# Moving transposes of a four-layer graph network from TensorE to HBM round trips, and scalings from VectorE to GpSimd

## The chip, the cores and the metric

One core of a Trainium2 chip runs the whole program. The metric is the time of one execution in microseconds (us), the median of several runs. All runs told here are of the fast state; the profile of each kernel is one further execution.

The engines are named as the profile names them: PE is TensorE (PEld its weight loads), DVE is VectorE, ACT is ScalarE, POOL is GpSimd, SP is SyncE. SPq and ACTq are the queues from which SP and ACT issue DMAs.

## The reference

Sixteen graphs (a "batch" below is one of them) of 1024 nodes with 128 features, one 1024x1024 adjacency matrix each, go through four layers, each of them `x = x + layer(relu(layernorm(x)))`.

```python
# layer 0, three times: h = h @ W + b; nh = h / |h|
#   h = (adj * (nh @ nh.T)) @ h, with relu but for the last
# layer 1: two matmuls around adj.T @ h
# layer 2:
h = x @ W;  s1 = h @ a[:f];  s2 = h @ a[f:]
alpha = tanh(s1[:, :, None] + s2[:, None, :])
attn = softmax(where(adj > 0, alpha, -1e15), axis=-1);  out = attn @ h
# layer 3: e = (h @ A) @ h.T, made symmetric; softmax over adj > 0, times adj;
#   then gates: z = sigmoid(i * h' + f * x);  out = o * tanh(z)
```

## The kernel before

The kernel records operations with estimated durations and latencies, and a list scheduler puts them in order, engine by engine, by priorities that were tuned by hand or by search (`LEADS`). Each engine then takes its instructions strictly in that order. Two or three batches are in work at once.

```python
# the scheduler's latency from an operation's end to its users, us
LATENCY = {"PE": 0.2, "DVE": 0.185, "ACT": 0.2, "POOL": 0.12, "DMA": 4.0}

# layers 0 and 3: one row of blocks of a symmetric product
pc, view = square.row(j, s)        # PE: above the diagonal matmuls, below it transposes of kept blocks
... scalar_tensor_tensor(ew, pc * rn * aT[j]) ...     # DVE reads PSUM
square.keep(j, s, pc)              # ACT (or DVE) copies the blocks that are mirrored later

# layer 2: the score s1 along the free axis, on all partitions
for s, (lo, hi) in enumerate(HALVES):
    p1 = ps(f"p1_{b}_{s}")
    # four transposes of h's score column, broadcast to 128 columns, then an eviction by ACT
    nc.tensor.transpose(cols(p1.t, c - lo), h.t[:, at : at + 1].to_broadcast([P, P]), ident)
    evict(p1, s1, lo, hi)
# the score's column is then used again, for the softmax's sums
dve(TINY, [], [h], lambda: nc.vector.memset(by_block(h.t, E2)[:, :, D : D + 1], 1.0))
for j in range(NB):
    act(..., lambda: nc.scalar.activation(e.t, s1.t, AF.Tanh, bias=<score s2 of node block j>))
    ...

# layer 3: exp of a row times the adjacency, on DVE in two halves
nc.vector.tensor_mul(span(e.t, lo, hi), span(e.t, lo, hi), span(aT[j].t, lo, hi))
```

Of the kernel before, what the change touches and what calls it, by code (L numbers as in the profile page):

```python
# [53 lines left out]
class Plan:  # L54
# [53 lines left out]
    def link(self):  # L108



        for o in self.ops:
            for b in [b for b in o.new if b.kind == "ps"]:
                for r in b.users:
                    if r is not o:
                        for t in [t for t in r.new if t.kind not in self.psum]:
                            r.new.remove(t)
                            o.new.append(t)
        behind = {o: set(o.preds) for o in self.ops}
        for o in self.ops:  # L120
            for b in o.new:
                for u in b.users:
                    if u is not o:
                        self.place_after(u, o)
                        behind[u].add(o)
        for o in self.ops:
            for b in [b for b in o.new if b.kind in self.psum]:
                for u in b.users:
                    for p in behind[u]:
                        if p.seq < o.seq:  # L130
                            self.place_after(o, p)
        for o in reversed(self.ops):
            o.tail = o.us + max((s.tail + o.lat for s in o.succs), default=0.0)
            o.rank = (self.deadline(o.batch) - o.tail - self.leads.get(o.key, 0.0), o.seq)
# [87 lines left out]
def tile_adj_preln(  # L222
# [97 lines left out]
    for load_it in first:  # L320
# [11 lines left out]
    POOLS = {"adjT": 16, "adjL": 5, "x": 3, "big": 13, "above": 2, "got": 1, "bank": 8, "small": 24, "row": 5, "hbm": 3}  # L332
    KINDS = {
        "adjT": ("adjT", 16, 16), "adjL": ("adjL", 5, 5), "x": ("x", 3, 3), "w4": ("big", 9, 8),
        "chunk": ("big", 10, 4), "above": ("above", 2, 1), "got": ("got", 1, 1), "ps": ("bank", 4, 4),
        "acc": ("bank", 8, 5), "small": ("small", 16, 6), "row": ("row", 5, 5), "hbm": ("hbm", 3, 2),
    }
    PERIOD, LAST, AHEAD, WINDOW = 66.0, 23.0, 2, 0.05

    LEADS = {  # L340
        "0 ACT hT": 3.5, "0 ACT hn": 18.5, "0 DVE hn": 14.5, "0 DVE nb": -43.5, "0 DVE st": -4, "0 PE ps": 13.5,
        "0 POOL rstd": -24, "00 ACT above": 74, "00 ACT hTn": -86, "00 ACT params": -0.5, "00 ACT sq": 49,
        "00 DMA by": 16.5, "00 DMA got": 16.5, "00 DVE above": -7.5, "00 DVE ew": 1, "00 DVE h": -224.5,
        "00 DVE params": 64.5, "00 DVE ss": 12.5, "00 PE acc0": -62, "00 PE ps": 81.5, "00 PE psP": 523.5,
        "00 PE sq": -15, "00 POOL rn": -26.5, "01 ACT above": 69, "01 ACT hT": 19, "01 ACT hTn": -158,
        "01 ACT sq": 4.5, "01 DMA by": 18.5, "01 DMA got": 31, "01 DVE above": 1.5, "01 DVE ew": 316.5,
        "01 DVE h": 20, "01 PE ps": 12, "01 PE psP": 27, "01 PE sq": 55.5, "01 POOL rn": 19, "02 ACT above": -1,
        "02 ACT hTn": -32, "02 ACT sq": -30.5, "02 DMA by": 21, "02 DVE above": -1, "02 DVE ew": -53.5,
        "02 DVE h": 3, "02 DVE ss": -403, "02 DVE x": -30, "02 PE acc0": -29.5, "02 PE ps": -131.5,
        "02 PE psP": 13, "02 PE sq": -24.5, "02 POOL rn": 20, "1 DMA adjL": -497, "1 DVE adjL": 4.5,  # L350
        "1 DVE hn": 238, "1 DVE mv": 35.5, "1 DVE nb": -17, "1 DVE st": -449, "1 DVE x": -3.5,
        "1 PE acc1": -32.5, "1 PE py": -31.5, "1 PE py2": -32, "1 POOL rstd": -28, "2 ACT e2": -33.5,
        "2 ACT h": 2, "2 ACT hfl": -64, "2 ACT hn": -370, "2 ACT hnT": -5.5, "2 ACT s1": 1.5,
        "2 DVE alone": -36, "2 DVE e2": 5.5, "2 DVE h": -125.5, "2 DVE hn": 74.5, "2 DVE hrow": 5,
        "2 DVE mv": 60, "2 DVE nb": 263.5, "2 DVE rden": 23, "2 DVE st": 153, "2 DVE x": 18.5, "2 PE p1": -18,
        "2 PE pf": -240.5, "2 PE ps": -21, "2 PE psP": -186, "2 POOL rstd": -12.5, "3 ACT above": -206,
        "3 ACT e3": -111.5, "3 ACT gT": -84, "3 ACT gate": 81.5, "3 ACT h3T": -30.5, "3 ACT hn": -79,
        "3 ACT hnT": 243, "3 ACT hp": -80.5, "3 ACT hpT": 102.5, "3 ACT hs": -38.5, "3 ACT z": -290.5,
        "3 DMA by": 49, "3 DMA z": 1.5, "3 DVE e3": -89, "3 DVE gate": 68.5, "3 DVE h": -14.5, "3 DVE hn": 4.5,
        "3 DVE nb": -41, "3 DVE st": -5.5, "3 DVE sum": -15.5, "3 DVE z": -618, "3 PE acc3": -42.5,  # L360
        "3 PE pg": -27, "3 PE ps": 23, "3 PE psN": -301.5, "3 PE psP": -25, "3 PE sq": -17.5,
        "3 POOL rstd": -23.5, "3 POOL z": 3.5, "T DMA adjT": -143, "T DVE adjT": -223.5, "x DMA x": -51,
# [4 lines left out]
    def op(engine, us, reads, writes, fn, port=False, lat=None):  # L367
        o = plan.op(engine, us, reads, writes, fn, now[0], port, lat)
        t = (list(writes) + list(reads))[0]
        o.key = f"{now[1]} {engine} {(t[0] if isinstance(t, tuple) else t).name.split('_')[0]}"  # L370
        return o
# [4 lines left out]
    def act(us, reads, writes, fn):  # L376
        return op("ACT", us, reads, writes, fn)

    def dve(us, reads, writes, fn, port=False):
        return op("DVE", us, reads, writes, fn, port)  # L380
# [27 lines left out]
    FAR = range(1, B - 2)  # L408
# [37 lines left out]
    def flip(src, lo, hi, dst, w=D):  # L446
# [6 lines left out]
        pe((hi - lo) * TR, [blk(src, lo, hi, w)], [dst], emit)  # L453

# [59 lines left out]

    def layernorm(k, xt, behind=None):
# [47 lines left out]

        lo, hi = HALVES[0]
# [5 lines left out]
    def relu(t):  # L570

        lo, hi = HALVES[0]
# [120 lines left out]
    def load(b):  # L693
        xt = Buf("x", [P, N], f"x_{b}")
        op(
            "DMA", 2.2, [], [xt],
            lambda: nc.sync.dma_start(by_block(xt.t), x[b].rearrange("(c p) d -> p c d", p=P)),
        )
# [41 lines left out]
    def layer0(b, xt, aT, prepared):  # L740
        now[1] = "0"
        hn = layernorm(f"{b}_0", xt)
        hT = flipped(hn, f"hT_{b}_0", AF.Relu)
        rn = None
        for i in range(3):
# [18 lines left out]
            hTn = flipped(h, f"hTn_{k}")  # L764
            ss = small(f"ss_{k}", NB)
            sq = w4(f"sq_{k}")
            for lo, hi in HALVES:
# [15 lines left out]
            square = Square(k, hTn, hTn, b in FAR)  # L783
            acc = [bank(f"acc0_{k}_{s}") for s in range(2)]
            for j in range(NB):
                ew = chunk(f"ew_{k}_{j}")
                for s, (lo, hi) in enumerate(HALVES):
                    pc, view = square.row(j, s)
                    o = dve(
# [7 lines left out]
                    square.keep(j, s, pc)  # L797
# [15 lines left out]
    def layer1(b, xt, prepared):  # L813
# [6 lines left out]
        add_scaled(xt, D, 0, NB, b12, 0, 0, maskT, m, xt, True)  # L820
# [30 lines left out]
    def layer2(b, xt, aT, su):  # L851
# [10 lines left out]
        add_scaled(xt, D, 0, NB, hn, 0, D, alone, 0, xt, True)  # L862
# [25 lines left out]
        s1 = w4(f"s1_{b}")  # L888
        for s, (lo, hi) in enumerate(HALVES):
            p1 = ps(f"p1_{b}_{s}")  # L890
# [50 lines left out]
    def layer3(b, xt, aT):  # L941
# [3 lines left out]
        hnT = flipped(hn, f"hnT_{k}", AF.Relu)  # L945
        relu(hn)
        gT = w4(f"gT_{b}")
        for s, (lo, hi) in enumerate(HALVES):
            p = ps(f"pg_{b}_{s}")
            wide(p, wg, hnT, lo, hi)  # L950
            evict(p, gT, lo, hi, AF.Identity, bg)
# [12 lines left out]
        hT = flipped(h, f"h3T_{b}", w=E3)  # L964
        square = Square(k, gT, hT, b in FAR)
        acc = [bank(f"acc3_{b}_{s}") for s in range(2)]
        for j in range(NB):
            e = chunk(f"e3_{b}_{j}")
            for s, (lo, hi) in enumerate(HALVES):
                p, view = square.row(j, s)  # L970
                dve(
# [7 lines left out]
                square.keep(j, s, p)  # L979
# [12 lines left out]
            for lo, hi in HALVES:  # L992
# [29 lines left out]
        gate = small(f"gate_{b}", 3 * NB)  # L1022

        def of(g, n=NB):
            return gate.t.rearrange("p (g c) -> p g c", g=3)[:, g, :]

        dve(
            TINY, [hp, h], [gate],
            lambda: nc.vector.tensor_add(
                gate.t.rearrange("p (g c) -> p c g", g=3),  # L1030
                by_block(hp.t, E3)[:, :, D:], by_block(h.t, E3)[:, :, D:],
            ),
            True,
        )
        act(0.22, [gate], [gate], lambda: nc.scalar.activation(gate.t, gate.t, AF.Tanh, scale=0.5))
        dve(
            TINY, [gate], [gate],
            lambda: nc.vector.tensor_scalar(gate.t, gate.t, 0.5, 0.5, op0=ALU.mult, op1=ALU.add), True,
        )
        z = w4(f"z_{b}")  # L1040
        pool_op(
            1.9, [hn, gate], [z],
            lambda: nc.gpsimd.tensor_mul(by_block(z.t), by_block(hn.t), per_node(of(1))),
        )
        add_scaled(z, D, 0, NB, hp, 0, E3, gate, 0, z, True)

        def squash():
            v = z.t[:, 0:N]
            nc.scalar.activation(v, v, AF.Tanh, scale=0.5)
            nc.scalar.activation(v, v, AF.Tanh, scale=0.5, bias=half)  # L1050

        act(S(N) + S(N, True), [z], [z], squash)
        add_scaled(z, D, 0, NB, z, 0, D, gate, 2 * NB, xt, True)
        op(
            "DMA", 2.0, [z], [],
            lambda: nc.scalar.dma_start(out[b].rearrange("(c p) d -> p c d", p=P), by_block(z.t)),
        )
# [77 lines left out]
    with tc.manual_schedule():  # L1135
        for o in ordered:
            for t in o.new:
                src = psum if t.kind in plan.psum else hbm if t.kind == "hbm" else pool
# [36 lines left out]
```

## Time and profile before

| | before |
|---|---|
| time, us | 2484.5 (2483.9 to 2487.3, 4 runs) |
| PE / DVE / ACT / POOL busy, us | 2411 / 2119 / 1287 / 214 |
| one batch in the middle, us | 150.0 |
| last projection to the end, us | 14.6 |

The third row, called the period below, is the distance from one batch's power operation of a layernorm on GpSimd to the next batch's. The last row, called the tail, runs from the end of the last matmul to the end of the span. Both are worked out in the prediction, which also has the lines that tell what bounds the kernel.

### The profile page before, as it was taken

To read this page: it belongs to the slowest core of one execution; us is meant where nothing else is said; L and a number is where in the kernel's file an instruction comes from. 1 tells how busy PE (TensorE), PEld (TensorE's weight loads), DVE (VectorE), ACT (ScalarE), POOL (GpSimd) and SP (SyncE) were. 2 spreads that over 40 slices of the span, in tenths; PEclk is the share of its full clock that TensorE was granted. 3 is DMA by queue.
4 is the path that set the end of the run, shared out by engine and by line. 5 is a ranking of instruction groups with operands and counts; after the bars stand their busy time and mean duration, and the time that the engine had idled before them with its cause. 6 is when DMAs were issued, how large, how long until landed. Compare 5 with 4: busy or idle time off the path is not lost.

```text
span 2481.8 us, 34726 instructions
## 1 busy us (share of the span) xinstructions
PE 2410.6 (97%) x11946; PEld 1588.7 (64%) x11946; DVE 2119.4 (85%) x5278; ACT 1287.1 (52%) x2401; POOL 214.4 (9%) x134
## 2 busy tenths in 40 slices
PE   6999999999999999999999999999999999999987
PEld 3567566675766657566675766756566575765763
DVE  6767989898897989889898897988989899796777
ACT  4425554644646455454554636456454655554575
POOL 1000010010101011011010100101011010010100
PEclk9999999999999999999999999999999999999998
DMA  7622827648284563936648276473945638054100
GB/s 125 129 67 69 163 59 143 138 80 167 60 160 121 99 140 84 165 91 127 129 94 178 52 154 135 84 154 68 165 107 111 136 85 162 1 108 80 35 1 18
DMA packets 1129441, 263.35 MB, mean 106 GB/s; under 512 B 971824, under 2 KB 1112880, under 8 KB 1129264
## 3 DMA queue, kind: packets, MB, share of 16 engines
q1 hardware_dynamic: 1108352, 251.73, 50.0%
q10 hardware_dynamic: 20912, 9.40, 1.4%
q8 instruction: 94, 1.54, 0.3%
q14 instruction: 83, 0.68, 0.1%
HBM read 198.14 MB, written 62.91 MB: 105 GB/s over the span
## 4 chain that ended last, share of the span: by engine, by line
PE 78%; DVE 9%; ACT 7%; issue 2%; DMA 1%; SPq 1%; ACTq 0%; POOL 0%; POOLq 0%; DVEq 0%
PE acc L671 31%; PE sq L609 17%; PE acc L682 11%; PE psP L461 6%; PE sq L619 4%; ACT e L906 3%; DVE ew L791 3%; ACT e L910 3%; PE py L844 2%; PE py L471 2%; DVE e L914 2%; PE ps_hTn L451 1%; DVE z L505 1%; PE pg L471 1%; PE ps_hnT L451 1%
## 5 line engine op out<-in xcount | busy, mean ns | idle before, releaser
L791 DVE SCALAR_TENSOR_TENSOR ew<-sq,rn,adjT 128x512 f32<-128x512 f32 x612 | 436.9, 739 | 68.2 <-PE sq L619 32.0
L671 PE MATMUL acc<-ew,h 128*128 128x512 f32 x1024 | 480.6, 597 | 4.7 <-DVE ew L791 4.5
L609 PE MATMUL sq<-hTn 128*128 128x512 f32 (+3 forms) x1152 | 441.3, 489 | 0.4 <-ACT hTn L483 0.4
L641 ACT COPY above<-sq 128x384 f32<-128x384 f32 (+3 forms) x432 | 169.2, 394 | 403.9 <-DVE ew L791 366.5
L671 PEld LDWEIGHTS acc<-ew,h 128*128 128x128 f32 x1024 | 178.9, 191 | 174.0 <-issue 112.9
L609 PEld LDWEIGHTS sq<-hTn 128*128 128x128 f32 x1152 | 193.5, 191 | 124.0 <-issue 76.1
L682 PEld LDWEIGHTS acc<-h,e 128*128 128x128 f32 x2048 | 241.0, 192 | 29.3 <-DVE e L914 11.8
L682 PEld LDWEIGHTS acc<-h,ew 128*128 128x128 f32 x2048 | 240.8, 192 | 21.0 <-DVE ew L791 11.4
L444 POOL TENSOR_TENSOR rstd<-ve,mhalf 128x8 f32<-128x8 f32 x64 | 104.8, 1637 | 1725.7 <-DVE ve L536 1694.9
L682 PE MATMUL acc<-h,ew 128*128 128x128 f32 x2048 | 252.7, 276 | 0.4 <-DVE ew L791 0.4
L682 PE MATMUL acc<-h,e 128*128 128x129 f32 x2048 | 249.5, 277 | 2.8 <-DVE e L914 1.5
L671 PE MATMUL acc<-e,hs 128*128 128x512 f32 x512 | 240.6, 595 | 1.7 <-DVE e L995 1.7
L671 PE MATMUL acc<-adjL,hn 128*128 128x512 f32 x512 | 239.0, 595 | 0.1
L988 ACT ACTIVATE e<-e,top 128x1024 f32<-128x1024 f32 x128 | 147.1, 1149 | 173.0 <-DVE top L984 172.5
L735 ACT ACTIVATE adjT<-adjT 128x1024 f32<-128x1024 f32 x128 | 135.0, 1055 | 194.0 <-DVE adjT L732 163.7
L619 PEld LDWEIGHTS sq<-ident,above 128*128 128x128 f32 x960 | 125.7, 141 | 142.2 <-issue 74.0
L619 PE MATMUL sq<-ident,above 128*128 128x128 f32 x960 | 174.4, 275 | 27.8 <-ACT above L641 27.8
L914 DVE SCALAR_TENSOR_TENSOR e<-adjT,e 128x512 f32<-128x512 f32 x256 | 162.0, 683 | 41.9 <-ACT e L910 41.9
L732 DVE STREAM_TRANSPOSE adjT<-adjT 128x1024 f32<-128x1024 f32 x128 | 155.2, 1225 | 17.8 <-DMA adjT<-in_adj_dram 10.9
L995 DVE TENSOR_TENSOR e<-e,adjT 128x512 f32<-128x512 f32 x256 | 166.2, 680 | 0.0
L906 ACT ACTIVATE e<-s,h 128x1024 f32<-128x1024 f32 x128 | 143.1, 1141 | 38.4 <-issue 36.6
L631 DVE STREAM_TRANSPOSE above<-sq 128x512 f32<-128x512 f32 x208 | 147.0, 707 | 10.5 <-PE sq L609 9.1
(124 smaller groups left out, 3455.9 us busy)
## 6 DMA issues: line engine op xcount, KB each, us to landing
adjT<-in_adj_dram SPq DMA_DIRECT2D x512, 128.0 KB, 3.7
adjL<-in_adj_dram SPq DMA_DIRECT2D x128, 512.0 KB, 4.9
by_hbm<-above SPq DMA_DIRECT2D x104, 512.0 KB, 3.2
got<-by_hbm SPq DMA_DIRECT2D x416, 128.0 KB, 3.0
x<-in_x_dram SPq DMA_DIRECT2D x16, 512.0 KB, 5.3
out_dram<-z ACTq DMA_DIRECT2D x16, 512.0 KB, 3.3
b<-in_L_gnn_b_dram ACTq DMA_DIRECT2D x4, 64.0 KB, 3.8
w<-in_L_gnn_W_dram ACTq DMA_DIRECT2D x2, 128.0 KB, 3.8
```

The costliest lines, as they stand in the source:

```text
L461: nc.tensor.matmul(dst.t[:, (c - lo) * n : (c - lo + 1) * n], cols(srcT.t, c), w, start=True, stop=True)
L609: lambda: nc.tensor.matmul(dst.t[:, (first - lo) * P :], cols(leftT.t, j), span(rightT.t, first, hi), start=True, stop=True),
L619: nc.tensor.transpose(cols(dst.t, r), cols(above.t, p), ident)
L641: lambda: nc.scalar.copy(span(above.t, p, p + hi - first), read.t[:, (first - lo) * P :]),
L671: lambda s=s, lo=lo, hi=hi: nc.tensor.matmul(acc[s].t, cols(h.t, at, w), span(ew.t, lo, hi), start=(j == 0), stop=(j == NB - 1)),
L682: nc.tensor.matmul(a.t[:, (c - lo) * n : (c - lo + 1) * n], cols(ew.t, c), h.t[:, j * w : j * w + n], start=(j == 0 and c == lo), stop=(j ...
L732: dve(V(N), [t], [t], lambda t=t: nc.vector.transpose(t.t, t.t), True)
L791: lambda view=view, ew=ew, rn=rn, j=j, lo=lo, hi=hi: nc.vector.scalar_tensor_tensor(by_block(span(ew.t, lo, hi), D, 4), view(), rn.t[:, j ...
L906: lambda e=e, j=j: nc.scalar.activation(e.t[:, 0:N], s1.t[:, 0:N], AF.Tanh, bias=h.t[:, j * E2 + D + 1 : j * E2 + D + 2]),
L914: lambda e=e, j=j, lo=lo, hi=hi: nc.vector.scalar_tensor_tensor(span(e.t, lo, hi), span(aT[j].t, lo, hi), 0.0, span(e.t, lo, hi), op0=ALU. ...
L988: lambda e=e, top=top, tot=tot: nc.scalar.activation(e.t[:, 0:N], e.t[:, 0:N], AF.Exp, bias=top.t, accum_out=tot.t),
L995: lambda e=e, j=j, lo=lo, hi=hi: nc.vector.tensor_mul(span(e.t, lo, hi), span(e.t, lo, hi), span(aT[j].t, lo, hi)),
```

## The change

Its intent is to take work from the two busiest engines: transposes from PE, whose results could be had by a round trip through HBM in squares of 32 and a transpose on DVE, and multiplications and additions from DVE, which go to an almost idle GpSimd. The kept blocks are copied before the product reads PSUM, the last batch is finished in halves, the first input is loaded in halves, and all priorities and some pool sizes are new. (A "flip" is the transposed copy of a tile; `got` is a row of kept blocks that comes back mirrored from HBM.) Cut to its core:

```diff
+    FLAGS = set("Cabcdkxh5PSD4")
-    PERIOD, LAST, AHEAD, WINDOW = 66.0, 23.0, 2, 0.05
+    PERIOD, LAST, AHEAD, WINDOW = 94.0, 10.0, 2, 0.05
     LEADS = { ... }                                  # all new, separate for the first and last two batches
 # D: layer 0's first flip, batches 2 to 15
-        hT = flipped(hn, f"hT_{b}_0", AF.Relu)       # 8 PE transposes, 2 ACT evictions
+            relu(hn)
+            hT = squares(hn, f"hT_{b}_0")            # write to HBM, 4 reads in squares, DVE transpose
 # k: in layers 0 and 3
+                    if "k" in FLAGS:
+                        square.keep(j, s, pc)        # before the product, not after it
 # P: layer 2's and layer 3's scalings
+        pool_op(1.9, [a, scalar], [a], lambda: nc.gpsimd.tensor_mul(v(), v(), per_node(of_node())))
+        pool_op(1.9, [a, b], [dst], lambda: nc.gpsimd.tensor_add(by_block(dst.t), v(), by_block(b.t)))
 # S: layer 2's score, batches 0 to 13
+            def put():
+                with nc.allow_non_contiguous_dma(reason="one score of a node"):
+                    nc.sync.dma_start(sd.t.rearrange("c p -> p c"), by_block(h.t, E2)[:, :, D])
+            op("DMA", 0.8, [h], [sd], put, lat=2.2)
+            op("DMA", 2.2, [sd], [s1],
+                lambda: nc.sync.dma_start(s1.t[:, 0:N], sd.t.rearrange("c p -> (c p)").partition_broadcast(P)),
+                lat=2.4)
 # 5: layer 3's odd rows
+                pool_op(1.96, [e, aT[j]], [e], lambda e=e, j=j: nc.gpsimd.tensor_mul(e.t[:, 0:N], e.t[:, 0:N], aT[j].t))
```

## The prediction

> **What bounds the kernel now.** I read four views, in this order: the page's table of busy shares, the table of stretches, PE's waits, and the timeline of one stretch of PE.
>
> ```profile
> span 2481.8 us, 34726 instructions
> ...
> PE 2410.6 (97%) x11946; PEld 1588.7 (64%) x11946; DVE 2119.4 (85%) x5278; ACT 1287.1 (52%) x2401; POOL 214.4 (9%) x134
> ```
>
> PE looks full, but a pipelined matmul counts as busy while it only drains, so 97% does not say that PE runs at its own pace. The table of stretches cuts the span into a start, one period of the middle (the power operation on GpSimd recurs every 150.01 us, at 1018.43, 1168.44 and 1318.45, so one batch of 16 takes 150.0 us) and an end. Its columns are the stretch, its length, the busy time of PE, PE's weight loads, DVE, ACT and POOL, PE's clock, DMA share and GB/s.
>
> ```profile
> 0.00:62.00 62.00, 42.79 (x154) 24.60 (x155) 37.43 (x104) 25.34 (x50) 8.93 (x11) 0.92 0.79 125
> ...
> 1018.43:1168.44 150.01, 148.10 (x734) 97.35 (x733) 133.66 (x333) 78.78 (x147) 13.36 (x8) 1.00 0.58 120
> ...
> 2400.00:2482.00 82.00, 59.27 (x258) 36.46 (x256) 66.61 (x161) 44.46 (x87) 5.43 (x3) 0.85 0.05 13
> ```
>
> The reader is to see three regimes. In the middle PE is idle 1.9 us of 150. At the start it is idle 19.2 us of 62, and at the end 22.7 us of 82, where DVE is the busiest engine (66.6 us). PE's waits over the whole run:
>
> ```profile
> PE sq L619 <- ACT above L641: 27.8, 18, 2.0
> PE ps_hT L451 <- DVE hn L553: 10.3, 1, 10.3
> PE acc L671 <- DVE ew L791: 4.5, 3, 3.0
> ```
>
> The first is the only wait of the middle: the mirrored transposes of the symmetric product wait, 18 times, for ACT's copy of the blocks above the diagonal, 1.7 us each batch. The second is the first layernorm, before PE has any work. The timeline tells whether PE's busy time is real work:
>
> ```profile
> 1091.17 1.88 PE L671 MATMUL acc<-ew,h 128*128 128x512 f32 x4
> 1092.89 9.86 PE L682 MATMUL acc<-h,e 128*128 128x129 f32 x80
> 1102.59 1.02 PE L609 MATMUL sq<-hTn 128*128 128x512 f32 x2
> ...
> 1107.29 0.33 PE L619 MATMUL sq<-ident,above 128*128 128x128 f32 x1 [1.70 <-ACT above L641]
> ...
> 1117.86 1.04 PE L451 MATMUL ps_hT<-ident,hn 128*128 128x128 f32 x8
> 1118.73 0.60 PE L451 MATMUL ps_hTn<-ident,h 128*128 128x128 f32 x4
> ```
>
> From one start to the next: four records of 512 columns take 1.72 us (0.43 us each), 80 of 129 columns take 9.70 us (0.121 us), 8 transposes take 0.87 us (0.109 us). Taking those paces, with the number of records per batch, I get 55 us for the 128 records of line 671, 31 for line 609, some 30.5 for the 256 of line 682, 12.3 for 112 transposes, 11.3 for line 461, and 9 for the rest: about 149 us of a period of 150. So the middle is bound by PE at its own pace, plus that one wait.
>
> **What the Trainium skill says.** "TensorE: Matmul & The Clock Gate", Part 4: PE-mode transpose, says that a transpose on TensorE is a matmul against an identity, about 275 ns in a kernel, whose result must be copied out of PSUM. The trace agrees on the latency (273 ns for one alone) but in a run of eight each costs only 0.109 us, and that is what a removed one is worth. "GPSIMD Engine Reference", section 3.1, has GpSimd 1.96 times slower than VectorE on an addition of two tensors; here GpSimd's multiplication of 128x1024 takes 1897 ns against two VectorE halves of 680 ns: 1.4 times. "SBUF — State Buffer", section Who interferes with whom, says that a VectorE instruction with two SBUF inputs and a GpSimd instruction that reads SBUF block each other for a whole instruction. I found no such overlap with a large GpSimd operation in the trace of before, so no run here shows it yet. "DMA: Bandwidth & Descriptors", Specifications, puts line rate at 512 bytes and more; here 971824 of 1129441 packets are smaller, and they land 3.0 to 3.7 us after issue all the same.
>
> **The change part by part.**
>
> Layer 0's first flip (batches 2 to 15, 14 of them). Removed: 8 transposes and two ACT evictions. PE: 14 x 8 x 0.109 = 12.2 us. ACT: two evictions of 0.59 us less one new ReLU of 0.63 us. Added: a write to HBM (3.2 us to landing, from the row of `by_hbm<-above`), four reads in squares of 32 (3.0 us, row of `got<-by_hbm`) plus issue, and a VectorE transpose of 1024 (1.2 us). That is 9 to 10 us of latency in place of about 2; two or three batches are in work at once, so I take it as hidden.
>
> Layer 2's score (batches 0 to 13, 14 of them). Removed: 8 transposes and two evictions of 0.61 us. PE: another 12.2 us. The two DMAs cost some 7 us of latency, again beside other work.
>
> Both are on the bound itself, in its PE-bound stretch: 24.4 us, the one certain gain, 1.0%.
>
> GpSimd takes over odd rows and scalings. VectorE per batch loses 4 rows x 2 x 0.65 = 5.2 us, and 24 scale-and-adds of 0.27 us = 6.5 us, and gains the 1.2 us transpose: 133.7 becomes about 123 us of 150. GpSimd per batch gains 4 x 1.95 + 6 x 1.9 = 19 us: 13.4 becomes 33 us. In the middle VectorE is not the bound, so this is worth nothing by itself there; it makes waits rarer.
>
> Kept blocks copied first. PSUM is read by one engine at a time here: before, VectorE's product (0.74 us) ran ahead of ACT's copy (0.48 us), and the transpose waited for both. Now the copy comes first and the product later by about as much. The 1.7 us per batch can shrink to nothing or come back elsewhere, as PE then waits for the product. I take half: 0.85 x 16 = 14 us.
>
> Start. The first input is loaded in two halves; the first layernorm can begin some tenths of a us sooner, but weights and adjacency blocks arrive one after the other as before. I take 2 us.
>
> End. VectorE bounds it. Batches 14 and 15 give 8 odd rows to GpSimd: 8 x 1.3 = 10.5 us less on VectorE, so PE's last matmul should come some 10 us earlier. Then the tail. Before, 14.6 us pass from the last projection (2467.2) to the end. In the built program the GpSimd queue ends with three whole operations for batch 14, ten half-sized for batch 15 and two whole ones for batch 14, all after batch 14's last projection, which now stands directly before batch 15's on PE. That is 5 x 1.9 + 10 x 1.0 = 19.5 us (a half taken as half of 1.9, an estimate), plus eviction, gates and the output DMA: about 25 us. So the tail grows by some 9 us and eats the 10.
>
> Sum: 24.4 + 14 + 2 + 1 = 41 us; 2484.5 - 41 = 2443 us, a gain of 1.7%.
>
> **The rivals.**
>
> The first: every wait goes and both ends shrink too. All priorities were chosen anew, with separate ones for the first two and last two batches, and one more PSUM user may run at a time. For it: the start and end hold 42 us of PE idle time, and a wait of 27.8 us is addressed directly. Against it: the tail in GpSimd's queue. It would give 24 + 28 + 10 = 62 us: about 2422 us.
>
> The second: GpSimd's port becomes a new wait. Its 19 added us per batch stand against a VectorE that is still busy 123 us of 150, a good part of it with two SBUF inputs (lines 914, 995, the `got` half of 791). If a quarter of the GpSimd operations hold VectorE up for 1 us each, that is 2.5 us per batch, still less than VectorE gained; but a late product of layer 0 or 3 lets PE wait. It would use up the second gain and some of the first: 2460 to 2470 us.
>
> The third: a transfer is not hidden. Sync issues its DMAs in order, so a read of the flipped tile that waits for its write keeps adjacency loads behind it. For it: VectorE waited for adjacency blocks at the start (10.9 us over the run). Against it: DMA engines are half busy in the middle (0.58), and one more 512 KB in small packets stands beside some 8 MB per batch. It would cost 1 to 2 us per batch and leave about 2465 us.
>
> **Range and chances.** PE's work alone puts a floor under the middle: 150.0 - 1.75 - 1.7 = 146.6 us per batch, which without any gain at the ends means about 2433 us. Faster by over 2% means below 2436 us: nearly all waits gone, or a gain at the ends. I give that 0.32. Slower by over 2% would need a transfer or the port to cost 6 us per batch: 0.02. The rest, 0.66, is within 2%. The range is 2422 to 2464 us.
>
> **What would show it.** Right: PE has 224 transposes fewer (11722 records and about 24 us less), a period of 147 to 148.5 us, no or half the wait of the mirrored transposes, VectorE near 1950 us, POOL near 500 us, and over 20 us from the last projection to the end, all on GpSimd and ACT. Wrong: if the period stays near 150, the PE time was not on the path, or a new wait took its place (it should then stand in PE's list as the product, the flipped tile or the score). If VectorE's multiplications of odd and even rows show times well over 0.68 us, the port is shared at a cost. If the tail is near 15 us, my reading of GpSimd's last operations is wrong. If the period falls under 146, I have taken PE's pace for a floor that it isn't.

## The result

| | before | after |
|---|---|---|
| time, us | 2484.5 | 2597.2 (2595.9 to 2598.8, 4 runs) |
| PE records | 11946 | 11722 |
| DVE / POOL busy, us | 2119 / 214 | 2099 / 590 |
| one batch in the middle, us | 150.0 | 157.1 to 160.6 |
| last projection to the end, us | 14.6 | 25.9 |

The changed kernel is slower: ratio 1.045, 95% interval 1.043 to 1.047. Ratios here are the mean time of one kernel's fast runs over that of the other's of the same rounds, so not quite the ratio of the medians.

The page of the changed kernel, its first lines, and PE's waits:

```profile
span 2595.4 us, 34421 instructions
...
PE 2422.8 (93%) x11722; PEld 1583.0 (61%) x11722; DVE 2098.5 (81%) x4782; ACT 1283.9 (49%) x2362; POOL 589.6 (23%) x299
```

```profile
PE acc L819 <- DVE ew L956: 86.8, 29, 6.9
PE acc L830 <- DVE e L1106: 21.1, 24, 4.6
PE acc L830 <- DVE ew L956: 12.1, 12, 5.0
...
PE sq L767 <- ACT above L789: 1.1, 3, 0.6
```

The wait for the kept blocks went from 27.8 us to 1.1 us, as intended. In its place PE waits 120 us for DVE (the first three lines), up to 6.9 us at a time, although DVE is less busy than before. What DVE was doing then is seen in the timeline of one such place (columns: start, length, engine, line, operation; in brackets the idle time before it and what ended it):

```profile
1117.67 0.38 SPq L1071 DMA_DIRECT2D sd<-h  x1
...
1118.93 0.17 DVE L943 TENSOR_SCALAR ss<-ss 128x8 f32<-128x8 f32 x1
...
1127.08 0.17 DVE L1241 TENSOR_TENSOR gate<-hp,h 128x24 f32<-128x24 f32 x1 [7.97 <-issue]
1127.09 0.33 SPq L1076 DMA_DIRECT2D s<-sd  x1
1127.11 0.07 DVE L1092 MEMSET h<- 128x8 f32 x1
1127.17 0.74 DVE L956 SCALAR_TENSOR_TENSOR ew<-sq,rn,adjT 128x512 f32<-128x512 f32 x1
...
1127.97 1.76 PE L819 MATMUL acc<-ew,h 128*128 128x512 f32 x2 [5.06 <-DVE ew L956]
```

DVE stands for 8 us and starts again within 0.01 us of the moment when SP issues the score's second transfer, that is, when the first has landed. The memset in that group writes the ones into the column from which this first transfer reads the score; in the program's order it stands directly ahead of the gate and waits for that DMA. The profile puts the wait on the gate, as "issue": it had no releaser to show. In one other place, of 5.8 us, it names the memset itself as waiting for this transfer; that the other waits are the same is shown by run e1 below. Behind the memset, in DVE's order, stands a product of layer 0 for which PE waits. Over the run these waits ahead of the gate are 92.4 us in 11 places.

Such a stall costs PE more than its own length. These are three stretches around the same place: before the stall, after it, and later (columns as in the table of stretches in the prediction; the clock is the third from the end):

```profile
1118.00:1122.90 4.90, 4.90 (x24) 2.89 (x22) 0.86 (x2) 2.57 (x7) 1.65 (x1) 1.00 0.10 1
...
1128.30:1131.60 3.30, 3.30 (x6) 1.58 (x5) 2.78 (x5) 0.00 (x0) 0.00 (x0) 0.50 0.52 199
1131.70:1140.00 8.30, 7.94 (x34) 4.62 (x33) 7.82 (x10) 7.57 (x8) 5.58 (x3) 1.00 0.86 170
```

After 5.06 us without work PE is granted half its clock for some 3.4 us. The trace shows the same after each of the 16 stalls of PE of 3.8 us and more (half the clock for 3.4 to 6.8 us each, the first one longer). The kernel before has no stall of 3 us and outside its start and end no half clock.

The score's transfer itself:

```profile
L1071 SPq DMA_DIRECT2D sd<-h x14: 377/377/378, 195.9 to 2210.2; - x14
...
DMA to landing us min/median/max: 8.7/9.2/11.2
```

It moves 4 KB, and takes 9.2 us (the median) from its issue until it has landed; the plan had it at 0.8 + 2.2 = 3.0 us. The second transfer takes 4.9 us; the plan had 4.6.

A second thing changed. These are groups of the kernel before (busy us, mean ns), then those of the changed kernel that answer to them:

```profile
L914 DVE SCALAR_TENSOR_TENSOR e<-adjT,e 128x512 f32<-128x512 f32 x256 | 162.0, 683 | 41.9 <-ACT e L910 41.9
...
L984 DVE TENSOR_REDUCE top<-e 128x1 f32<-128x1024 f32 x128 | 154.3, 1205 | 0.2
...
L791 DVE SCALAR_TENSOR_TENSOR ew<-got,rn,adjT 128x512 f32<-128x512 f32 x156 | 112.8, 743 | 1.8
```

```profile
L1106 DVE SCALAR_TENSOR_TENSOR e<-adjT,e 128x512 f32<-128x512 f32 x256 | 202.9, 847 | 23.0 <-ACT e L1102 22.8
...
L1185 DVE TENSOR_REDUCE top<-e 128x1 f32<-128x1024 f32 x128 | 153.2, 1206 | 0.3
...
L956 DVE SCALAR_TENSOR_TENSOR ew<-got,rn,adjT 128x512 f32<-128x512 f32 x156 | 157.7, 1039 | 26.5 <-DMA got<-by_hbm 22.6 <-issue 3.7
```

The operation with two inputs in SBUF rose from 683 to 847 ns, and the one that reads `got` and the adjacency from 743 to 1039 ns; the reduction, with one input, and the product that reads one of its two large inputs from PSUM (739 and 738 ns) did not change. One case in the timeline:

```profile
1108.13 2.89 DVE L956 SCALAR_TENSOR_TENSOR ew<-got,rn,adjT 128x512 f32<-128x512 f32 x1
1108.13 2.35 POOL L655 TENSOR_TENSOR x<-hn,x 128x1024 f32<-128x1024 f32 x1
```

Both start together; DVE's 0.74 us become 2.89, GpSimd's 2.35 and then some 0.5 more. This is the block that "SBUF — State Buffer", section Who interferes with whom, describes, now with its number.

### The profile page after: what moved, and what is told of

It is laid out like the page before. It is cut to its first block, busy times and chain, and to the rows that moved or that the text cites. A ratio compares the mean times of both kernels' runs of the same rounds, so it can differ in the third digit from the quotient of the medians.

```text
span 2595.4 us, 34421 instructions
## 1 busy us (share of the span) xinstructions
PE 2422.8 (93%) x11722; PEld 1583.0 (61%) x11722; DVE 2098.5 (81%) x4782; ACT 1283.9 (49%) x2362; POOL 589.6 (23%) x299
## 4 chain that ended last, share of the span: by engine, by line
PE 77%; DVE 11%; issue 4%; ACT 3%; DMA 3%; POOL 1%; SPq 0%; POOLq 0%; DVEq 0%; ACTq 0%
PE acc L819 30%; PE sq L757 16%; PE acc L830 15%; PE psP L597 5%; PE sq L767 3%; DVE ew L956 3%; DVE e L1106 2%; PE py L1018 2%; PE py L607 2%; PE ps_hTn L566 2%; DVE top L1185 1%; PE pg L607 1%; DMA sd<-h 1%; PE ps_hnT L566 1%; DVE above L779 1%
## 5 line engine op out<-in xcount | busy, mean ns | idle before, releaser
L819 PE MATMUL acc<-ew,h 128*128 128x512 f32 x1024 | 494.6, 611 | 87.0 <-DVE ew L956 86.8
L757 PE MATMUL sq<-hTn 128*128 128x512 f32 (+3 forms) x1152 | 447.4, 502 | 0.0
L757 PEld LDWEIGHTS sq<-hTn 128*128 128x128 f32 x1152 | 203.0, 197 | 141.0 <-issue 87.8
L830 PEld LDWEIGHTS acc<-h,ew 128*128 128x128 f32 x2048 | 246.1, 192 | 43.0 <-DVE ew L956 21.8
L1194 POOL TENSOR_TENSOR e<-e,adjT 128x1024 f32<-128x1024 f32 x64 | 158.7, 2480 | 476.7 <-ACT e L1189 354.7
L1106 DVE SCALAR_TENSOR_TENSOR e<-adjT,e 128x512 f32<-128x512 f32 x256 | 202.9, 847 | 23.0 <-ACT e L1102 22.8
L559 POOL TENSOR_TENSOR rn<-ss,mhalf 128x8 f32<-128x8 f32 x48 | 79.1, 1649 | 479.6 <-DVE ss L943 479.4
L884 DVE STREAM_TRANSPOSE adjT<-adjT 128x1024 f32<-128x1024 f32 x128 | 157.0, 1231 | 28.9 <-DMA adjT<-in_adj_dram 23.5
L956 DVE SCALAR_TENSOR_TENSOR ew<-got,rn,adjT 128x512 f32<-128x512 f32 x156 | 157.7, 1039 | 26.5 <-DMA got<-by_hbm 22.6
```

Of the source, the lines that this page charges most:

```text
L559: pool_op(1.64, [src], [dst], lambda: nc.gpsimd.tensor_tensor(dst.t, src.t, mhalf, op=ALU.pow))
L757: lambda: nc.tensor.matmul(dst.t[:, (first - lo) * P :], cols(leftT.t, j), span(rightT.t, first, hi), start=True, stop=True),
L819: lambda s=s, lo=lo, hi=hi: nc.tensor.matmul(acc[s].t, cols(h.t, at, w), span(ew.t, lo, hi), start=(j == 0), stop=(j == NB - 1)),
L830: nc.tensor.matmul(a.t[:, (c - lo) * n : (c - lo + 1) * n], cols(ew.t, c), h.t[:, j * w : j * w + n], start=(j == 0 and c == lo), stop=(j ...
L884: dve(V(N), [t], [t], lambda t=t: nc.vector.transpose(t.t, t.t), True)
L956: lambda view=view, ew=ew, rn=rn, j=j, lo=lo, hi=hi: nc.vector.scalar_tensor_tensor(by_block(span(ew.t, lo, hi), D, 4), view(), rn.t[:, j ...
```

## The experiments

There is a trap in testing such a kernel: any change to the recorded operations makes the scheduler order everything anew. Two runs below (e4 and b1) were ordered anew. All others keep the order of the changed kernel, and change only what an operation in it does. "Before" took 2486.2 to 2487.1 us (medians) beside these runs, which were made in three groups on three chips; "back" below is the difference from the 2597.2 us of the changed kernel.

**Theories.** A: the memset's wait for the score's transfer is the loss. B: the port shared by GpSimd and DVE is the loss.

### e1_scorecopy: the transfer reads a copy, so that the memset need not wait

```diff
+                    nc.scalar.copy(score[b % 3][:, lo:hi], by_block(pp.t, E2, hi - lo)[:, :, D])
-                    nc.sync.dma_start(sd.t.rearrange("c p -> p c"), by_block(h.t, E2)[:, :, D])
+                    nc.sync.dma_start(sd.t.rearrange("c p -> p c"), score[b % 3])
```

> The order of all other instructions stays as in the changed kernel; only the write of the ones column no longer waits for the score's DMA. Theory A (this wait stalls VectorE some 8 us per batch, and PE behind it): VectorE's unexplained waits ahead of the gate (92 us) go, PE's waits for the product of layer 0 (87 us) fall to under 30, and the time falls by 60 to 90 us to 2510 to 2540. Theory B (GpSimd holding the shared port is the main cost): less than 20 us come back, 2578 or more.

Measured: 2576.3 us, 21 us back. Neither theory's numbers hold. The two waits that theory A named fell as it said (DVE's ahead of the gate are gone, PE's for the product of layer 0 are 26.3 us), but the time did not follow: PE waits for the softmax instead, and ACT for the score. Of PE's waits in this run, then of ACT's:

```profile
PE acc L831 <- DVE e L1107: 68.2, 14, 7.0
PE acc L820 <- DVE ew L957: 26.3, 24, 7.0
```

```profile
ACT e L1099 <- DMA s<-sd: 106.8, 14, 11.9
```

In the changed kernel ACT waited 31.9 us for the score. The delay is the same; it has moved from DVE's queue to ACT's. So theory A as stated falls, and theory C takes its place: the whole round trip of the score is later than planned, and whoever stands behind it in order stalls.

### e2_trim and e3_both: GpSimd's added work on 8 columns (wrong result on purpose)

```diff
-  nc.gpsimd.tensor_mul(e.t[:, 0:N], e.t[:, 0:N], aT[j].t)
+  nc.gpsimd.tensor_mul(e.t[:, 0:8], e.t[:, 0:8], aT[j].t[:, 0:8])      # and so for the scalings
```

> Same order as the changed kernel, wrong result on purpose: GpSimd's added multiplications and additions work on 8 columns, so they hold the port for a moment only. Theory B: VectorE's e2 product returns from 847 to 683 ns, and most of the 113 us come back (2510 or less). Theory A: VectorE's durations return but the wait for the score's DMA stays, and the time falls by 20 to 45 us, 2552 to 2577.

> Both of the above. If the two causes explain the loss, the time is 2450 to 2475, below the kernel before, as the 224 fewer transposes promise. If something else (the flip through HBM, transfers behind each other in Sync's queue, the kept blocks first) costs, it stays above 2484.

Measured: 2546.6 us for the trimmed kernel, 51 us back: less than theory B wants, more than a side effect. The group that had risen to 847 ns is at 686 ns again, that of `got` at 745. With both edits 2540.5 us, 57 us back and still above 2484: the two causes as then stated did not explain the loss, which is what led to theory C.

### e4_noS and b1_keep: one part taken out, one part alone, with the scheduler at work

e4 takes the score's round trip out of the changed kernel (its flag removed); b1 adds only "kept blocks first" to the kernel before.

> The score again by PE transposes and ACT evictions; the scheduler orders anew. Theory A: like e1, less the 12 us of transposes: 2520 to 2550. Theory B: 2590 or more.

> The kernel before with the kept blocks copied first, nothing else; the scheduler orders anew with the old priorities. If copying first is good by itself: 2460 to 2480, with PE's wait for the copied blocks (27.8 us) gone. If it only moves the wait to the product: 2480 to 2500, with PE waiting for VectorE's product by about as much.

Measured: 2797.0 and 2709.0 us. Both expectations fail by far. PE's waits in b1 are for many different things, the largest 42.8 us for layer 0's product. I read this as a matter of the order: the priorities were tuned for one list of operations, and another list gets an order for which they were not. That was not tested, and the two runs are not used for or against any part. From here on only runs in the same order are used as evidence.

### e9_nohop, e10_nohop_trim and e11_noflip: the score's first transfer taken away

The score row is fetched from the adjacency matrix (a wrong score), in the same place of the same order.

```diff
-            op("DMA", 0.8, [h], [sd], put, lat=2.2)
+            op("DMA", 0.8, [h], [sd], lambda: None, lat=2.2)
-                lambda: nc.sync.dma_start(s1.t[:, 0:N], sd.t.rearrange("c p -> (c p)").partition_broadcast(P)),
+                lambda: nc.sync.dma_start(s1.t[:, 0:N], adj[b, 0, :].partition_broadcast(P)),
```

> Same order as the changed kernel, wrong result on purpose: the score row is fetched from the adjacency matrix, so the write of the score to HBM (9.2 us to landing, planned as 3.0) is gone, with VectorE's wait for it and Sync's. Theory C (the score's round trip through HBM is some 6 to 9 us later than planned, and whichever engine stands in order behind it, VectorE in the changed kernel, ACT in e1, stalls): 70 us or more come back against the changed kernel, 2525 or less, well under e1's 2576. Rival (the round trip is mostly hidden; the loss is spread over other waits): within 15 us of e1.

> The same with GpSimd's added work trimmed to 8 columns. If the score's round trip and GpSimd's share of the port are all of the loss: 2450 to 2480. If a third cause remains (flip through HBM, copies first): over 2490.

> As before, and layer 0's flipped tile is read from an input instead of from what was written, so that Sync no longer stands waiting for the normalised tile (18 us per batch) ahead of other transfers. If Sync's standing in line costs: 10 to 25 us less than the run without this. If not: within 5 us of it.

Measured: e9 2479.6 us, 118 us back. Its result still passes the comparison, so the tolerance does not guard the score; no weight is put on that. e10 2430.5 us, a ratio of 0.977 to before (0.976 to 0.979). The two edits add up: 51 us for GpSimd, 118 us for the transfer, 167 us for both. The period is 149.99 us in e9 and 147.15 us in e10. The 118 us are not idle time alone: with the same 11722 records PE is busy 2422.8 us in the changed kernel and 2387.0 us in e9, at a mean granted clock of 0.977 and 0.992. So some 36 us of them are matmuls at half the clock after the stalls (an estimate, as the ends of matmuls are modelled), the other 82 us less idle time of PE.

PE's waits in e9, then in e10 (each line: who waited for whom, us in total, times, longest):

```profile
PE acc L819 <- DVE ew L956: 22.1, 17, 7.1
PE acc L830 <- DVE e L1106: 14.6, 23, 4.4
```

```profile
PE acc L819 <- DVE ew L956: 9.5, 6, 6.1
PE acc L830 <- DVE ew L956: 6.8, 10, 0.7
PE acc L830 <- DVE e L1106: 4.2, 1, 4.2
```

So theory C holds, and GpSimd is a second cause of its own. e9 also takes away SP's standing in line for the score's write (131.1 us in the changed kernel), a rival. But DVE's waits for what SP fetches after it, adjacency blocks and `got`, stay as they were: 23.5 + 22.6 us in the changed kernel, 24.3 + 23.2 us in e9. So that is not what the 118 us are. e11, in which the flipped tile of layer 0 no longer depends on a write to HBM, takes 2430.7 us, as e10: the flip's round trip costs nothing that shows. It was not a clean test of SP standing in line for the flip, as SP stood about as long there, for other things.

### g1_rows32: the same score, correct, in fewer pieces

DVE copies the score to a 128x32 tile and turns it in squares of 32; the write to HBM is then 32 runs of 128 bytes instead of 1024 of 4. The order is again that of the changed kernel.

```diff
-                    nc.sync.dma_start(sd.t.rearrange("c p -> p c"), by_block(h.t, E2)[:, :, D])
+                nc.vector.tensor_copy(score[b % 3][:, 0:NB], by_block(h.t, E2)[:, :, D])
+                nc.vector.transpose(scoreT[b % 3], score[b % 3])
+                for g in range(P // SQ):
+                    nc.sync.dma_start(sd.t[:, g * SQ : (g + 1) * SQ], scoreT[b % 3][g * SQ : g * SQ + NB, :])
```

> Order of the changed kernel, correct result: the score is copied to a small tile and turned in squares of 32 by VectorE, so that 32 runs of 128 bytes go to HBM instead of 1024 of 4 bytes. Theory C: the write lands in 2.5 to 4 us instead of 9.2, near the plan, and the time is within 20 us of the run without the write (2480): 2480 to 2500. If the number of pieces is not what makes the write slow, it stays above 2540.

Measured: 2483.9 us, 113 us less than the changed kernel and 4 us more than e9. It passes the comparison; as e9 passes it too, that the score is right rests on reading the edit. SP's timeline shows the second transfer 2.66 us after the first was issued, where it was 9.42 us (2.3 to 3.4 and 8.8 to 11.3 us over the 14 batches):

```profile
1065.29 1.32 SPq L1077 DMA_DIRECT2D sd<-scoreT  x4
1067.95 0.35 SPq L1082 DMA_DIRECT2D s<-sd  x1
```

### g2_odd, g3_p and g4_all: GpSimd's parts back on DVE, one by one

The operation keeps its place in the order and is issued on DVE: the odd rows as one multiplication of 1024 (g2), the scalings as eight multiply-and-adds of 128 as before the change (g3), both (g4).

```diff
-  nc.gpsimd.tensor_mul(e.t[:, 0:N], e.t[:, 0:N], aT[j].t)          # g2, g4
+  nc.vector.tensor_mul(e.t[:, 0:N], e.t[:, 0:N], aT[j].t)
-  nc.gpsimd.tensor_mul(...); nc.gpsimd.tensor_add(...)             # g3, g4
+  for k in range(lo, hi): nc.vector.scalar_tensor_tensor(...)
```

> The same, and the odd rows' multiplication issued on VectorE at the place that the plan gives GpSimd's. Theory B' (GpSimd's port costs 49 us as the difference of two runs with the score's write gone shows, and the odd rows, 159 of its 410 added us, are the part that meets VectorE most): 15 to 30 us less than g1. If VectorE's own added 78 us cost as much: no less than g1.

> The same as g1, with the scalings (not the odd rows) on VectorE: 15 to 30 us less than g1 by theory B', and the tail after the last projection back to some 15 us.

> The same as g1 with both on VectorE, correct: the best version so far if theory B' holds, 2435 to 2460, under the 2486 of before. If VectorE becomes the bound instead: 2470 or more.

| | time, us | ratio to before | period, us |
|---|---|---|---|
| g1: odd rows and scalings on GpSimd | 2483.9 | 0.999 | 150.0 |
| g2: scalings on GpSimd | 2509.4 | 1.009 | 152.1 |
| g3: odd rows on GpSimd | 2459.1 | 0.989 (0.987 to 0.991) | 148.1 |
| g4: neither | 2484.3 | 0.999 | 150.2 |

My expectation for g2 was the wrong way round: the odd rows are better on GpSimd, by 25 us. The scalings are better on DVE, by 25 us. Some 8 us of this are the tail, which is 25.6 us in g1, with the scalings on GpSimd, and 17.5 us in g3; the rest is in the period. g3 is the fastest version found that passes the comparison, 1.1% faster than the kernel before and 5.3% than the changed one.

The traces also tell which part meets DVE. First g2 (scalings on GpSimd), then g3 (odd rows on GpSimd):

```profile
L1112 DVE SCALAR_TENSOR_TENSOR e<-adjT,e 128x512 f32<-128x512 f32 x256 | 203.6, 850 | 20.1 <-ACT e L1108 20.0
L960 DVE SCALAR_TENSOR_TENSOR ew<-got,rn,adjT 128x512 f32<-128x512 f32 x156 | 163.8, 1078 | 21.6 <-DMA got<-by_hbm 20.4
```

```profile
L1119 DVE SCALAR_TENSOR_TENSOR e<-adjT,e 128x512 f32<-128x512 f32 x256 | 162.7, 686 | 21.5 <-ACT e L1115 20.6
```

The two products that had slowed down are slow with the scalings on GpSimd, and as fast as before with the odd rows there (`got`: 745 ns in g3). The theory had it the other way round. In sum, against g4 with 2129.5 us of DVE busy, moving the odd rows to GpSimd leaves DVE 2091.4 us (g3), and moving the scalings leaves it 2146.5 us (g2): the block took back more than the scalings had freed.

## Why the prediction was wrong

The prediction was 2443 us and within 2%; the result is 2597 us. Step by step:

**The first step that failed: "The two DMAs cost some 7 us of latency, again beside other work."** Both halves are wrong. The latency is 9.2 + 4.9 = 14.1 us, and it isn't hidden: the order is fixed by a plan that has 7.6 us, and DVE's and ACT's queues are in order. I gave the 7 us without working; the landing times that I had looked at, 3.0 to 3.7 us, are of transfers in runs of 128 bytes and more, and this one is 1024 runs of 4 bytes. I also did not ask who writes what the transfer reads: the memset stood in the kernel before. Shown by e9 (118 us back, 8.4 us for each of the 14 batches) and g1 (113 us back). A transfer that costs 6 us per batch is what I had given a chance of 0.02. The third rival had named a transfer that is not hidden, but that of the flip, at 1 to 2 us per batch and through SP's queue. e11 shows no cost of the flip, and e1 that the stall went through DVE's queue first and through ACT's when that was cleared. Its figures for the traffic were off as well, without consequence: the pages give 263.35 MB before, some 16 MB per batch and not 8, and 22 MB more after. No part of the prediction has PE's clock in it; the stalls also halved that.

**The second: "In the middle VectorE is not the bound, so this is worth nothing by itself there."** GpSimd's share was put at no cost in the sum and at 2.5 us per batch in the second rival. With the score out of the way it costs 149.99 - 147.15 = 2.84 us per batch and, with the tail (25.6 against 13.6 us), 49 us in all (e9 less e10). So the second rival had the mechanism and nearly the size, and I left it out of the sum. Of the signs that I named, two failed here: DVE was to be near 1950 us and POOL near 500; they are 2099 and 590, and with GpSimd's added work trimmed DVE is at 1962 us (e10). A term under it was mis-sized too: I took 1.95 us for an odd row from the multiplication by a broadcast gate; with two whole inputs it takes 2.35 us even at its fastest and 2.48 us on average.

**Right: the count of transposes, and the floor.** PE has 11722 records, as told; that they were worth 24.4 us was not isolated by a run. The prediction put the floor of the middle at 146.6 us per batch and about 2433 us in all; with both costs out, e10 has 147.15 us and 2430.5 us. That the total agrees so closely is partly luck: the period is 0.55 us above the floor, and the ends, in which no gain was counted, made up for it. PE's own pace, from the starts of records in the timeline, was a sound base for what could be won in the middle.

**Right in part: kept blocks first.** PE's wait for them fell from 27.8 to 1.1 us. I took half as a gain, the other half coming back as waits for the product. In e10 those are 16.3 us (9.5 + 6.8), against 4.9 in the kernel before. So about half came back, though no run isolates this part.

**Right: the tail.** From the last projection to the end I expected about 25 us; it is 25.9 us, with the GpSimd operations in the order in which the built program has them. The end of the changed kernel:

```profile
2567.09 2.40 PE L597 MATMUL psN<-eye,hpT 128*128 128x131 f32 x20
...
2569.37 1.91 POOL L1252 TENSOR_TENSOR hp<-hp,gate 128x1024 f32<-128x1024 f32 x1 [4.41 <-DVE gate L1266]
...
2588.52 2.34 POOL L1253 TENSOR_TENSOR z<-z,x 128x1024 f32<-128x1024 f32 x1
```

GpSimd works without a pause for 21.5 us after PE is done.

What stays open: how the 49 us divide between DVE being blocked and GpSimd's results coming later than planned (the trimmed runs remove both), and what a new search of priorities with the true durations would find.

## What to carry to other kernels

Price a transfer by the number of its pieces, not only by its bytes, and find out who writes the memory that it reads: a small write on an in-order engine can stand behind it. Count a stall of PE at more than its length: here half the clock followed each of the long ones. Ask of work that is moved to GpSimd which operations of DVE it will run beside; DVE's busy time, which contains the block, tells whether it was relieved. When a wait is removed and the time hardly moves, look for the same delay in the next queue before giving up the theory; the test that settles it takes the delay itself away. Where a scheduler makes the order, test parts in the same order, since adding or removing a part there also tests an untuned order.

## What the Trainium skill lacked or had wrong

- "DMA: Bandwidth & Descriptors", Rules for kernel authors, says that a non-contiguous last dimension becomes one descriptor per element and advises to rearrange; that row gives no cost. Here 4 KB as 1024 pieces of 4 bytes took 9.42 us from the issue to the issue of the transfer that waits for it, and as 32 runs of 128 bytes in four transfers 2.66 us.
- "GPSIMD Engine Reference", section 3.1, has one figure for an addition of two tensors (4497 ns for 2048 elements, 2249 ns for 1024 as an estimate from it). It was nearer than my own reading: with two whole inputs the multiplication of an odd row of 1024 took at least 2347 ns, the one with an input broadcast along the row 1897 ns on average in the kernel before. The page doesn't tell the two forms apart.
- "SBUF — State Buffer", section Who interferes with whom: the block of a VectorE operation with two SBUF inputs agrees with the runs (0.74 us became 2.89 us beside a GpSimd operation of 2.35 us; the group's mean 683 became 847 ns; reductions with one input stayed at 1206 ns). It doesn't say how much of the time that is freed on VectorE the block takes back. Here VectorE's busy time went from 2129.5 to 2091.4 us when the odd rows were moved (25 us gained), and to 2146.5 us when the scalings were (25 us lost).
- "TensorE: Matmul & The Clock Gate", Part 4, gives a transpose's latency, not its pace: 273 ns alone, 0.109 us each in a run of eight.
